# The queries of the last attention block: made in that block from stored transposed rows, and no longer in the block before

## The chip, the cores and the metric

One Trainium2 chip, and on it one core. The time of a run is the device time of that core in microseconds. The kernel before took 2020.83 us, the median of 9 runs (2013.94 to 2037.01).

The names of the engines are those of the profile: PE multiplies matrices, PEld loads the stationary operand of a matmul, DVE is the vector engine, ACT the scalar engine with its table functions, POOL issues the indirect DMAs (gathers and scatters by an index list), SP issues plain DMAs. PSUM is the memory that PE writes to, in banks of 512 float32 per partition.

## The reference

A graph network of four layers on 3327 nodes with 256 features. `adj` is a random sparse matrix with ones on its diagonal; a node of this input has itself and at most 24 others as neighbours. Three of the layers are attention blocks, the second one is an average over neighbours.

```python
def _L3_gnn_ref(x, adj, w_qkv, w_proj, b_proj, w1, b1, w2, b2, g1, be1, g2, be2):
    qkv = layer_norm(x, g1, be1) @ w_qkv                 # [n, 768]
    qkv = qkv.reshape(n, 3, HEADS, HEAD_DIM)             # 8 heads of 32
    q, k, v = (qkv[:, 0], qkv[:, 1], qkv[:, 2])
    scores = jnp.einsum('nhd,mhd->hnm', q, k) * SCALE    # SCALE = 32 ** -0.5
    scores = jnp.where(adj != 0, scores, -jnp.inf)
    out = jnp.einsum('hnm,mhd->nhd', softmax(scores), v).reshape(n, DIM)
    x = x + out @ w_proj + b_proj
    ff = gelu(layer_norm(x, g2, be2) @ w1 + b1) @ w2 + b2   # 256 -> 1024 -> 256
    return x + ff

x = _L0_gnn_ref(x, adj, ...)   # attention
x = _L1_gnn_ref(x, adj, ...)   # h = x @ Wt.T; average of neighbours' h with softmax weights; norm
x = _L2_gnn_ref(x, adj, ...)   # attention
x = _L3_gnn_ref(x, adj, ...)   # attention
```

## The kernel before

The nodes, sorted by their number of neighbours, are cut into 26 tiles of 128 rows. Tile t has room for `ROOM[t]` neighbours per node, from 24 down to 4. The stages, with their places in the trace: neighbour lists out of `adj` (to about 280 us), the first attention block (to 720), the averaging layer (to 1021), the middle attention block (to 1553) and the last one (to the end). In the code the three attention blocks are `layer` 0, 1 and 2, and they run the same functions.

A block works tile by tile in the order written in `GROUPS[layer]`, in which one to four tiles make a group. For a tile, `attend` (L1282) does this:

- It loads the tile's own row of queries, keys and values into `own`, a part of a buffer `first`. In the last block that is a load on SP from the DRAM table `own[t]` (L1294).
- ACT copies the 256 query columns into `query`, half a PSUM bank (L1297). There are two such halves (`QS` is 2).
- POOL gathers keys and values of the neighbours, one indirect DMA per neighbour slot, four slots to a buffer (`first`, then `unit`s). DVE multiplies each buffer's keys by `query` and reduces them to `scores`. In the trace these are the groups `first<-first,query` and `unit<-unit,query`.
- ACT takes the exponential, DVE weights the values and adds them up in `acc` and then `o`, and PE transposes `o` into `turns`.

`project` multiplies by `w_proj` and adds to the rows `x`. A few tiles later `norm`, `turned` and `feed_forward` make `hT` (normed, transposed rows; a ring of two buffers, `HTS`), the sixteen w1 matmuls with their gelu `gT`, and the eight w2 matmuls of a tile. `end` closes the tile. In the last block it scatters the rows of `x` to the output. In the middle block it calls the `finish` of `into_keys` (L985), which makes what the last block needs: the next layer's norm and its transposed rows `hT`, two matmuls 512 wide for keys and values and a copy to `qkv`, two matmuls 256 wide for queries and a scaled write beside them (L1004 and L1005), a scatter of keys and values on POOL into the table from which the last block gathers, and a store of the whole row (768 float32) on SP to `own[t]` (L1010). A float32 matmul of the program appears in the trace as two, so that one tile's keys and values are four instructions of PE there, and its queries four more. `mm` is the ring of three PSUM banks that all these matmuls write to, and L402 and L406 are the lines of a helper through which all instructions of the blocks go, so that groups are told apart by their tiles' names.

The order on each engine is planned. The blocks' code only records operations (`Weave.record`); `order` (L289) then plays them through with a modelled duration for each, picks at each step the operation that can start first (of several, the one of the earlier tile), hands out the buffers of the rings, and adds a slack where an operation waits for another engine's: 8.0 us where DVE waits for PE (`SLACK` for tensor to vector), 1.0 for PE to ACT, 0.6 for ACT to DVE, and 0.1 for pairs that aren't listed. `emit` writes the operations in that order, and each engine then runs its own list in order, waiting where a semaphore says so.

The gathers of the last block wait for all scatters of the middle block (`held = making`).

Of the kernel before, what the change touches and what calls it, by code (L numbers as in the profile page):

```python
# [32 lines left out]
P = 128  # L33
CW = 512
N = 3327
DIM = 256
# [4 lines left out]
SCALE = HD**-0.5  # L41
# [11 lines left out]
KC = DIM // P  # L53
# [15 lines left out]
SLACK = {("tensor", "vector"): 8.0, ("tensor", "scalar"): 1.0, ("scalar", "vector"): 0.6, ("scalar", "gpsimd"): 6.0, ("vector", "gpsimd"): 6.0, "unit": 2.0, "first": 2.0}  # L69
# [25 lines left out]
OTS, HTS, XHS, OS, QKVS = 2, 2, 3, 4, 2  # L95
# [89 lines left out]


class Op:
    __slots__ = ("spots", "lane", "method", "args", "kw", "then", "rank", "needs", "busy", "done", "table", "n", "moves", "alone")


class Weave:
# [33 lines left out]
    def record(self, lane, method, args, kw, then, alone, also):  # L225
        op = Op()
        op.lane, op.method, op.args, op.kw, op.then = lane, method, args, kw, then
        op.n = len(self.ops)
        op.rank, op.alone = self.rank, alone
        op.moves = False  # L230
# [24 lines left out]
        self.cost(op, *plain)  # L255
        self.ops.append(op)
        return op
# [31 lines left out]
    def order(self):  # L289
        ops = self.ops  # L290
# [12 lines left out]
        ready = [0.0] * len(ops)  # L303
# [25 lines left out]
        table, flights, starts, clock = 0, [], {}, Clock()  # L329
        while len(starts) < len(ops):  # L330
            best = None
            for lane in LANES:
                can = []
                for n in wait[lane]:
                    t = opening(ops[n])
# [16 lines left out]
            op = ops[pick]  # L352
# [24 lines left out]
            for n in users[pick]:  # L377
                left[n] -= 1
                same = ops[n].lane == lane
                end = free[lane] if same and lane == "tensor" else ends[pick]  # L380
                ready[n] = max(ready[n], end + (0.0 if same else SLACK.get((lane, ops[n].lane), 0.1)))
                if not left[n]:
                    wait[ops[n].lane].append(n)
        self.starts, self.length, self.at = starts, max(ends), at
# [27 lines left out]
class Sparse:  # L412
# [572 lines left out]
    def into_keys(self, layer, w_qkv, g1, be1):  # L985

        def then(b):
            w = b.w
            made = []
            rows = b.ring("qkv", [P, 3 * DIM], QKVS)  # L990

            def begin():
                b.keys = self.fetch_keys(w_qkv, g1, be1, w)

            def finish(group, sums):
                wq, g, be = b.keys
                hT = b.turned(group, sums, g, be)
                out = []
                for q, t in enumerate(group):
                    r = rows()  # L1000
                    kv, qq = b.mm(), b.mm()
                    w.tensor.matmuls(kv, [(hT[:, k, ts(q, P)], wq[:, k, DIM : 3 * DIM]) for k in range(KC)])
                    w.scalar.copy(r[:, : 2 * DIM], kv)
                    w.tensor.matmuls(qq[:, :DIM], [(hT[:, k, ts(q, P)], wq[:, k, :DIM]) for k in range(KC)])  # L1004
                    w.scalar.mul(r[:, 2 * DIM :], qq[:, :DIM], SCALE)  # L1005
                    w.gpsimd.indirect_dma_start(
                        out=self.places[layer], out_offset=bass.IndirectOffsetOnAxis(ap=self.half[t], axis=0),
                        in_=r[:, : 2 * DIM], in_offset=None, then=lambda ins: self.apart(ins, made), alone=True,
                    )
                    w.sync.dma_start(out=self.own[t], in_=r)  # L1010
                return out

            self.making = made
            return begin, finish, None

        return then
# [238 lines left out]
class Block:  # L1255
# [26 lines left out]
    def attend(self, t):  # L1282
# [11 lines left out]
            w.sync.dma_start(out=own[:, : 3 * DIM], in_=L.own[t])  # L1294
        query = self.query()
        s = self.scores()[:, : (J + 1) * HEADS].rearrange("p (j h) -> p j h", h=HEADS)
        w.scalar.copy(query, own[:, 2 * DIM : 3 * DIM])  # L1297
        units = []
        held = L.held
        for j0 in range(0, J, UNIT):  # L1300
# [165 lines left out]
    def run(self):  # L1466
        w = self.w
        later = []

        def call(now):  # L1470
            while later and (now is None or later[0][0] <= now):
                at, stage, group, rank, made = later.pop(0)
                w.rank = rank
                if stage == 1:
                    later.append((at + DELAY[1], 2, group, rank, self.feed_forward(group, made)))
                    if self.ahead and group == sum(GROUPS[self.layer][-1], ()):
                        self.ahead(w)
                else:
                    self.end(group, made)
                later.sort(key=lambda x: (x[0], -x[1]))  # L1480

        step = 0
        for squad in GROUPS[self.layer]:
            group = sum(squad, ())
            sums = self.small["sums"]()
            for pair in squad:
                outs = []
                for t in pair:
                    w.rank = step
# [546 lines left out]
```

## Time and profile before

| | |
|---|---|
| median of the 9 runs | 2020.83 us |
| all runs | 2013.94, 2015.85, 2018.14, 2018.59, 2020.83, 2032.62, 2036.69, 2036.99, 2037.01 |
| the profiled execution | 2015.0 us, its span 2013.3 us |
| mean granted clock of TensorE | 0.791 |
| busy in the span | PE 1262.9 us (63%), DVE 1374.5 (68%), POOL 982.3 (49%), PEld 852.3 (42%), ACT 728.3 (36%) |
| the middle block, 1022 to 1553 (531 us) | PE 362.8, DVE 366.6, ACT 234.1, POOL 241.0 |
| the last block, 1553 to 2013 (460 us) | PE 288.8, DVE 347.4, ACT 146.0, POOL 244.5 |

The busy time of an engine is the time in which it executes; PEld runs beside PE. The granted clock is the share of full speed at which the throttle lets TensorE run. In a group of instructions, the numbers after the bar are busy time, mean nanoseconds of one, and the idle time of the engine just before these instructions with what ended it. In a line of waits, the instruction left of the arrow waited for the one right of it: total us, times, longest. In the timeline a line is one instruction, with its start, its duration and, in brackets, what it had waited for.

### The profile page before, as it was taken

To read this page: it belongs to the slowest core of one execution; us is meant where nothing else is said; L and a number is where in the kernel's file an instruction comes from. 1 tells how busy PE (TensorE), PEld (TensorE's weight loads), DVE (VectorE), ACT (ScalarE), POOL (GpSimd) and SP (SyncE) were. 2 spreads that over 40 slices of the span, in tenths; PEclk is the share of its full clock that TensorE was granted. 3 is DMA by queue.
4 is the path that set the end of the run, shared out by engine and by line. 5 is a ranking of instruction groups with operands and counts; after the bars stand their busy time and mean duration, and the time that the engine had idled before them with its cause. 6 is when DMAs were issued, how large, how long until landed. Compare 5 with 4: busy or idle time off the path is not lost. (4 is left out here: it accounts for less than half of the span.)

```text
span 2013.3 us, 18004 instructions
## 1 busy us (share of the span) xinstructions
PE 1262.9 (63%) x5126; PEld 852.3 (42%) x5126; DVE 1374.5 (68%) x3500; ACT 728.3 (36%) x1575; POOL 982.3 (49%) x977
## 2 busy tenths in 40 slices
PE   3335513575765587899924776877687157578775
PEld 1112201252434345666512454555465043345554
DVE  5999338776756792256737786878661699788882
ACT  5654211323323243032312453554454134144332
POOL 6998456556454422011165445545401666656530
PEclk9667755677887688899866888988789577788787
DMA  8987396555454453474486556556513666655620
GB/s 297 374 334 279 119 324 196 169 172 159 147 175 130 139 121 103 110 218 154 190 308 219 175 187 208 189 174 203 156 58 134 208 195 207 206 164 182 166 84 13
DMA packets 166245, 369.77 MB, mean 184 GB/s; under 512 B 75629, under 2 KB 87123, under 8 KB 162808
## 3 DMA queue, kind: packets, MB, share of 16 engines
q0 software_dynamic: 68624, 222.01, 35.6%
q1 hardware_dynamic: 86279, 115.85, 17.2%
q10 hardware_dynamic: 11232, 30.68, 4.1%
q8 instruction: 42, 0.69, 0.1%
q14 instruction: 68, 0.56, 0.1%
HBM read 279.77 MB, written 77.59 MB: 178 GB/s over the span
## 5 line engine op out<-in xcount | busy, mean ns | idle before, releaser
L406 POOL DMA_INDIRECT unit<-kv,ids x372 | 352.6, 948 | 292.8 <-issue 97.5
L402 PE MATMUL mm<-hT,w 128*128 128x256 f32 (+2 forms) x1280 | 343.0, 423 | 138.7 <-issue 64.4
L406 POOL DMA_INDIRECT first<-kv,ids x338 | 319.9, 946 | 212.1 <-issue 113.9
L402 PE MATMUL mm<-w,gT 128*128 128x256 f32 x1248 | 311.8, 403 | 50.6 <-issue 32.2
L402 PEld LDWEIGHTS mm<-hT,w 128*128 128x128 f32 x1280 | 225.3, 213 | 227.7 <-issue 123.1
L402 PEld LDWEIGHTS mm<-w,gT 128*128 128x128 f32 x1248 | 245.1, 202 | 98.7 <-issue 40.5
L406 ACT ACTIVATE gT<-mm,b 128x128 f32<-128x128 f32 (+2 forms) x320 | 133.3, 467 | 276.0 <-remote 163.3
L406 DVE TENSOR_TENSOR first<-first,query 128x1280 f32<-128x1280 f32 x78 | 115.3, 1478 | 142.3 <-DMA first<-kv,ids 58.1
L402 PE MATMUL mm<-wproj,oT 128*128 128x256 f32 x312 | 115.5, 503 | 73.2 <-issue 38.3
L406 PE MATMUL turns<-ident,o 128*128 128x128 f32 x156 | 40.4, 349 | 183.4 <-issue 91.7
L406 DVE TENSOR_REDUCE scores<-first 128x40 f32<-128x1280 f32 x78 | 116.2, 1489 | 41.3 <-ACT scores L406 28.1
L406 DVE SCALAR_TENSOR_TENSOR rows<-mm,rows 128x256 f32<-128x256 f32 x156 | 64.6, 416 | 102.9 <-remote 62.1
L406 DVE TENSOR_TENSOR unit<-unit,query 128x1024 f32<-128x1024 f32 (+3 forms) x120 | 115.7, 964 | 27.1 <-DMA first<-kv,ids 15.7
L406 DVE TENSOR_TENSOR acc<-acc,unit 128x512 f32<-128x512 f32 (+1 forms) x204 | 131.6, 645 | 1.6 <-DVE scores L406 1.4
L406 DVE TENSOR_REDUCE scores<-unit 128x32 f32<-128x1024 f32 (+3 forms) x120 | 117.6, 980 | 14.9 <-ACT scores L406 8.6
L959 PE MATMUL kvps<-wqkv,hT 128*128 128x512 f32 x208 | 110.9, 658 | 22.6 <-ACT st L962 9.7
L406 DVE TENSOR_TENSOR unit<-unit,scores 128x1024 f32<-128x1024 f32 (+3 forms) x120 | 116.3, 971 | 0.0
L406 ACT ACT_TABLE_LOAD x89 | 114.2, 1283 | 1.5
L1205 POOL DMA_INDIRECT sorted<-unit,to x26 | 24.8, 955 | 182.8 <-ACT unit L963 151.3
L402 PEld LDWEIGHTS mm<-wproj,oT 128*128 128x128 f32 x312 | 71.0, 247 | 98.3 <-issue 46.8
L674 DVE MAX8 found<-m 128x8 f16<-128x416 f16 x208 | 104.9, 577 | 10.4 <-POOL m L660 5.2
L406 PEld LDWEIGHTS turns<-ident,o 128*128 128x128 f32 x156 | 22.8, 173 | 202.4 <-issue 123.7
(215 smaller groups left out, 2211.4 us busy)
## 6 DMA issues: line engine op xcount, KB each, us to landing
a<-in_adj SPq DMA_DIRECT2D x25, 1663.5 KB
kv<-unit ACTq DMA_DIRECT2D x26, 512.0 KB
first<-sorted SPq DMA_DIRECT2D x26, 512.0 KB
own<-qkv SPq DMA_DIRECT2D x26, 384.0 KB
first<-own SPq DMA_DIRECT2D x26, 384.0 KB
kv<-st ACTq DMA_DIRECT2D x13, 512.0 KB
adj<-a SPq DMA_DIRECT2D x15, 416.0 KB
w<-in_L_gnn_w SPq DMA_DIRECT2D x6, 1024.0 KB
```

Of the source, the lines that this page charges most:

```text
L402: self.nc.tensor.matmul(out, real(left), real(right), start=k == 0, stop=k == len(pairs) - 1)
L406: ins = getattr(getattr(self.nc, op.lane), op.method)(*args, **kw)
L674: nc.vector.max(found[:, t, s, :], m[:, ts(s, SEG)])
L959: nc.tensor.matmul(kv, hT[:, k, ts(q, P)], w[:, k, DIM : 3 * DIM], start=k == 0, stop=k == KC - 1)
L1205: nc.gpsimd.indirect_dma_start(out=self.sorted[:], out_offset=bass.IndirectOffsetOnAxis(ap=self.to[:, c + q : c + q + 1], axis=0), in_=y, ...
```

## The change

The finish of the middle block makes keys and values only. The buffer `qkv` shrinks from 768 to 512 columns, the 256-wide matmuls and the scaled write go, and in place of one store of the row there are two: keys and values into the first 512 columns of `own[t]`, and the tile's part of `hT` into the last 256. What then lies in those columns is the transposed rows of the tile, cut into two halves of 128.

In the last block `attend` no longer copies the query. Two matmuls of the program (four in the trace) take the stored halves as stationary operand and the query part of `w_qkv` as moving one and write straight into the PSUM half `query`. The factor SCALE goes into those weights, by one multiplication on ACT that `run` records ahead of the last block's first tile. Each of these matmuls is marked `prompt`, and `order` then lets DVE follow after a slack of 0.1 instead of 8.0 us. The first two blocks copy their queries as before.

```diff
 class Op:
-    __slots__ = (..., "moves", "alone")
+    __slots__ = (..., "moves", "alone", "prompt")
...
@@ order
-                ready[n] = max(ready[n], end + (0.0 if same else SLACK.get((lane, ops[n].lane), 0.1)))
+                ready[n] = max(ready[n], end + (0.0 if same else 0.1 if ops[pick].prompt else SLACK.get((lane, ops[n].lane), 0.1)))
...
@@ into_keys
-            rows = b.ring("qkv", [P, 3 * DIM], QKVS)
+            rows = b.ring("qkv", [P, 2 * DIM], QKVS)
 
             def begin():
                 b.keys = self.fetch_keys(w_qkv, g1, be1, w)
+                self.wq = b.keys[0][:, :, :DIM]
...
-                    kv, qq = b.mm(), b.mm()
+                    kv = b.mm()
                     w.tensor.matmuls(kv, [(hT[:, k, ts(q, P)], wq[:, k, DIM : 3 * DIM]) for k in range(KC)])
-                    w.scalar.copy(r[:, : 2 * DIM], kv)
-                    w.tensor.matmuls(qq[:, :DIM], [(hT[:, k, ts(q, P)], wq[:, k, :DIM]) for k in range(KC)])
-                    w.scalar.mul(r[:, 2 * DIM :], qq[:, :DIM], SCALE)
+                    w.scalar.copy(r, kv)
...
-                    w.sync.dma_start(out=self.own[t], in_=r)
+                    w.sync.dma_start(out=self.own[t][:, : 2 * DIM], in_=r)
+                    w.sync.dma_start(
+                        out=self.own[t][:, 2 * DIM :].rearrange("p (k w) -> p k w", k=KC), in_=hT[:, :, ts(q, P)]
+                    )
...
@@ attend
-        w.scalar.copy(query, own[:, 2 * DIM : 3 * DIM])
+        if layer < 2:
+            w.scalar.copy(query, own[:, 2 * DIM : 3 * DIM])
+        else:
+            ask = w.tensor.matmuls(query, [(own[:, ds((2 * KC + k) * P, P)], L.wq[:, k, :]) for k in range(KC)])
+            ask.prompt = True
...
@@ run
+        if self.layer == 2:
+            w.scalar.mul(self.L.wq, self.L.wq, SCALE)
         for squad in GROUPS[self.layer]:
```

More of the change, by code (lines that the diff above doesn't have):

```diff
@@ L187 @@
 class Op:
-    __slots__ = ("spots", "lane", "method", "args", "kw", "then", "rank", "needs", "busy", "done", "table", "n", "moves", "alone")
+    __slots__ = ("spots", "lane", "method", "args", "kw", "then", "rank", "needs", "busy", "done", "table", "n", "moves", "alone", "prompt")
 class Weave:
@@ L229, in record @@
         op.rank, op.alone = self.rank, alone
-        op.moves = False
+        op.moves, op.prompt = False, False
         outs = [kw[k] for k in ("out", "accum_out") if kw.get(k) is not None]
@@ L1000, in finish @@
                     r = rows()
-                    kv, qq = b.mm(), b.mm()
+                    kv = b.mm()
                     w.tensor.matmuls(kv, [(hT[:, k, ts(q, P)], wq[:, k, DIM : 3 * DIM]) for k in range(KC)])
-                    w.scalar.copy(r[:, : 2 * DIM], kv)
-                    w.tensor.matmuls(qq[:, :DIM], [(hT[:, k, ts(q, P)], wq[:, k, :DIM]) for k in range(KC)])
-                    w.scalar.mul(r[:, 2 * DIM :], qq[:, :DIM], SCALE)
+                    w.scalar.copy(r, kv)
                     w.gpsimd.indirect_dma_start(
                         out=self.places[layer], out_offset=bass.IndirectOffsetOnAxis(ap=self.half[t], axis=0),
-                        in_=r[:, : 2 * DIM], in_offset=None, then=lambda ins: self.apart(ins, made), alone=True,
+                        in_=r, in_offset=None, then=lambda ins: self.apart(ins, made), alone=True,
                     )
-                    w.sync.dma_start(out=self.own[t], in_=r)
+                    w.sync.dma_start(out=self.own[t][:, : 2 * DIM], in_=r)
+                    w.sync.dma_start(
+                        out=self.own[t][:, 2 * DIM :].rearrange("p (k w) -> p k w", k=KC), in_=hT[:, :, ts(q, P)]
+                    )
                 return out
```

## The prediction

> **What bounds the kernel now.** I read the page first (span, stages, chain), then the busy time in windows over the last two attention blocks, then the timeline where they meet, then groups and waits. The profiled execution took 2015.0 us around a span of 2013.3; the median of the runs shown, 2020.83, is 5.8 above it (five runs lie at 2014 to 2021 with mean 2017.5, four at 2032 to 2037).
>
> The edit touches the middle block (from about 1022 us to 1553) and the last one (1553 to the end). Windows, columns PE, PEld, DVE, ACT, POOL busy us (instructions), granted clock, DMA share, GB/s:
>
> ```profile
> 1400.00:1450.00 50.00, 29.00 (x128) 21.85 (x126) 34.98 (x84) 16.46 (x42) 26.23 (x28) 0.83 0.55 170
> 1450.00:1500.00 50.00, 42.04 (x196) 31.45 (x197) 36.47 (x113) 29.97 (x79) 5.16 (x8) 0.86 0.27 90
> 1500.00:1553.00 53.00, 46.00 (x225) 32.89 (x223) 11.93 (x73) 26.13 (x77) 5.57 (x11) 0.97 0.30 107
> 1600.00:1650.00 50.00, 27.00 (x94) 18.58 (x94) 44.56 (x95) 16.14 (x35) 30.24 (x32) 0.70 0.65 208
> 1650.00:1700.00 50.00, 32.05 (x78) 15.64 (x78) 44.95 (x97) 18.38 (x39) 29.00 (x29) 0.68 0.57 177
> 1850.00:1900.00 50.00, 39.15 (x160) 30.13 (x159) 43.55 (x88) 16.64 (x36) 31.55 (x33) 0.87 0.61 168
> ```
>
> So two regimes. Inside a block DVE leads (44 of 50 us) and PE has a third of its time free. At the end of the middle block DVE has run dry (11.93 of 53) and PE is full (46 of 53). The timeline shows that end:
>
> ```profile
> 1488.51 0.42 DVE L406 TENSOR_TENSOR o<-acc,o 128x256 f32<-128x256 f32 x1
> ...
> 1503.68 0.27 PE L406 MATMUL turns<-ident,o 128*128 128x128 f32 x1
> ...
> 1541.95 2.85 PE L402 MATMUL mm<-wqkv,hT 128*128 128x512 f32 x8 [0.55 <-ACT hT L406]
> ...
> 1548.70 4.54 PE L402 MATMUL mm<-wqkv,hT 128*128 128x512 f32 x8 [0.55 <-ACT hT L406]
> ...
> 1552.79 0.96 POOL L406 DMA_INDIRECT kv<-qkv,ids  x1 [6.88 <-ACT qkv L406]
> ...
> 1556.52 0.98 POOL L406 DMA_INDIRECT first<-kv,ids  x1 [2.78 <-issue]
> ```
>
> The last attention row o is done at 1488.9, PE turns it only at 1503.7 (it is behind), and the last keys and values are scattered at 1552.8. The first gather of the last block waits for all scatters. These 63.9 us are on the path that sets the end. (x8 is one tile: four matmuls 512 wide for keys and values, four 256 wide for queries.)
>
> ```profile
> L402 PE MATMUL mm<-wqkv,hT 128*128 128x256 f32 x104 | 28.2, 394 | 2.1 <-ACT qkv L406 1.5 <-DVE acc L406 0.5
> L406 ACT ACTIVATE qkv<-mm 128x256 f32<-128x256 f32 x26 | 9.9, 379 | 21.6 <-remote 14.3 <-PE mm L402 7.0 <-issue 0.3
> L406 ACT COPY query<-first 128x256 f32<-128x256 f32 x43 | 16.3, 379 | 77.9 <-DVE unit L406 26.7 <-DVE first L406 13.4 <-issue 12.5
> ```
>
> The first two groups are what leaves the middle block; the third holds the copies that leave the last.
>
> **The change, part by part.**
>
> *Query matmuls leave the middle block.* A tile's eight matmuls take 2.85 us at the high clock; by width the queries are a third, 0.95. 26 tiles: 24.7 us of PE. Where PE has room this is worth nothing; in the tail it counts. I counted the PE instructions that stand, in the order of the two built programs, between the last o and the last key/value matmul, and priced them with tail rows (key/value tile 1.90, eight w2 matmuls 3.62, sixteen w1 matmuls 3.84, transpose 0.21, projection matmul 0.5, bias 0.28). Before: 6 key/value tiles, 6 query tiles, 4.5 x 3.62, 4 x 3.84, 18 transposes, 4 projections, 7 biases: 57 us, which took 63.9. After: 5 key/value tiles, 3.5 x 3.62, 3 x 3.84, 14 transposes, 2 projections, 5 biases: 39 us. That is 18 less; 5.7 are queries, the rest is feed-forward that now stands ahead of the last o. It has room there: PE work ahead of the last o also falls, from 284 to 277 us. Bounds: 6 if only the queries go (the surplus stands, but PE reaches it as late as now), 18 if all does. What is late next is the last tile's own chain (projection, norm, feed-forward, norm, keys), which doesn't shrink. I take 14, nearer the count, since in before the trace stood within a matmul or two of its listed order at the last o.
>
> *Scaled query writes leave ACT.* 26 x 379 ns = 9.9 us, about 19 of them ahead of the tail where ACT is 40 to 60% busy, each behind the key/value copy that the scatter needs, so not on the path. A PSUM bank per tile is also freed. Gain 0 to 7; counted 0.
>
> *Stores.* One 3 KB-row store per tile becomes two, 2 KB rows and two 512-byte runs per partition: 26 more SP issues at 0.32 us, 8.3 us on a queue that mostly waits (131.4 us for ACT qkv, 130.4 for DVE o). New is that hT is free only once its store has landed, and the store stands in SP's queue behind loads that wait for DVE (longest 25.4). The ring has two hT; who needs the next waits on ACT, and with it the exp behind. Bounds 0 to 12 (about half of that longest wait; the trace has no store of hT). In the tail the DMA is 30% busy and no such load stands between: 0. In the body DVE idles 87 us for many reasons now; I take 0 net with ACT's gain, range -7 to +12.
>
> *Scaling the weights.* One ACT pass over 128x512, 0.58 us like the copy of that shape. In the built order it stands on ACT at the start of the middle block, after the second query copy, waiting for the weight load. That load was issued at 1022.9, ahead of the tile load for which ACT idles 8.98 us until 1037.7. Cost 0; if the weights landed last, its 0.6.
>
> *Queries in the last block.* 26 x 379 ns leave ACT. PE gains 26 x 0.95 = 24.7 us at the high clock, 26 x 1.51 = 39 at the low one (4.54/3, the tile at 1548.70). PE has about 115 us free in 1600 to 1950, so its time alone costs nothing. The new wait is DVE's first multiply of a tile for PE, whose queue it shares with feed-forward. Cover: in the built order the DVE work between a query and its use is mostly 10 to 16 us, but 4 and 8 at the tenth and ninth tile and none at the last but one, where sixteen w2 matmuls stand ahead. Against that, ACT no longer stands at query copies:
>
> ```profile
> ACT query L406 <- DVE unit L406: 23.7, 6, 11.3
> ...
> ACT query L406 <- DVE first L406: 13.4, 2, 12.0
> ```
>
> PE stands there instead, though usually already behind a transpose of o. In this block DVE shows no stall over 1 us that ended with an ACT query, so nothing direct is won. The four first queries lie under the 8 us until the first gather lands. Bounds -10 (all of ACT's 9.9 us) to +25 (PE the bound); I take +4: 3 at the last but one, 1 at the tenth.
>
> The clock bears on this: it is granted at 0.97 in the tail that loses the matmuls, and at 0.70 and 0.68 in two windows that get them. The Trainium skill (TensorE: Matmul & The Clock Gate, Part 1) says that an idle window of some 3.4 us puts PE back at half rate, so it speaks against moving work from a dense to a sparse stage. The trace agrees in kind; by the rule alone every query would run cold and the sum would take the 39 us as PE's added load instead of 24.7, still inside PE's free time.
>
> *The prompt flag* only tells the planner that DVE may follow these matmuls after 0.1 instead of 8 us; its effect is the order counted above.
>
> **Sum.** 2015.0 - 14 + 0 + 4 = 2005 for an execution like the profiled one. Less 10, the lower group's mean gives 2007.5 and the median 2010.8; I forecast 2009.
>
> **Rivals.**
>
> *A, slower: PE's queue becomes DVE's start.* If PE runs more than one tile's cover (about 10.5 us of DVE work) behind its listed place, each tile of the last block begins with a wait. For it: PE waits of 11.4 us for gT in that block, and 15 us at the last block-1 rows turned. Against: PE is a third idle. Price, if PE paces all 26 tiles: 26 x 1.23 (midway between 0.95 and 1.51) = 32, less 14: +18, about 2036.
>
> *B, same: only the query matmuls leave the tail.* PE reaches the last o as late as now; -6, +4, and a few us for held hT: about 2019.
>
> *C, faster still.* ACT, free of copies that wait for DVE, serves gelu and exp sooner in both blocks: -18, -5 in the last block instead of +4: about 1995.
>
> *D, it does not do what it says*: queries are still made once per tile and no fewer matmuls run in all; that is so, and is why only their place counts.
>
> **How the numbers follow.** Forecast 0.50, A 0.21, B 0.18, C 0.11. About 0.5% (10 us) is what a measurement of this kernel tells from none. The forecast's own range is 2000 to 2018, so of its 0.50 some 0.37 is faster. With C and a little of B: faster 0.50. Same takes 0.13 from the forecast, most of B and 0.02 of A: 0.30. Slower 0.20. The range reaches from C to A: 1994 to 2035.
>
> **What would show it.** Right: no 256-wide wqkv matmuls in the middle block; last o to last scatter some 50 us instead of 64; 104 matmuls into query after it; DVE gaps before the first multiply of a tile ended by PE of 3 us or less, except at the last but one tile. Wrong: the scatter-to-end stretch (460 us) grown by more than 10; ACT hT waiting for a DMA of own; the last o much later than 1489.

## The result and the profile after

The changed kernel took 2050.91 us, the median of 20 runs (2041.11 to 2066.4), where the kernel before took 2024.47, the median of 62. The ratio is 1.016, with a 95% interval of 1.0139 to 1.0182: it is slower by 1.6%, some 32 us. (That ratio is of the means of the runs that count as fast, 2053.4 over 2021.0; the medians as they stand differ by 26 us.) The forecast was 2009, its range 1994 to 2035.

The profiled execution has a span of 2043.8 us against 2013.3. The trace can be cut at three events that both kernels have: the first and last attention row of the middle block, the last scatter of its keys and values, and the first and last attention row of the last block. (The events are the starts of DVE's second addition into o, and the start of the scatter, in the timeline.)

| us | before | after | difference |
|---|---|---|---|
| middle block, first o to last o | 439.7 | 450.6 | +10.9 |
| last o to last scatter | 64.3 | 52.3 | -12.0 |
| last scatter to first o of the last block | 24.2 | 24.5 | +0.3 |
| last block, first o to last o | 392.8 | 424.0 | +31.2 |
| last o to the end | 43.4 | 43.4 | 0 |

So the end of the middle block became shorter by about what was forecast, the same block lost nearly as much ahead of it, and the last block lost 31. The end of the middle block, in the timeline of the changed kernel (the same events as were shown of the kernel before):

```profile
1499.63 0.42 DVE L406 TENSOR_TENSOR o<-acc,o 128x256 f32<-128x256 f32 x1
...
1504.20 0.38 PE L406 MATMUL turns<-ident,o 128*128 128x128 f32 x2
...
1540.23 1.98 PE L402 MATMUL mm<-wqkv,hT 128*128 128x512 f32 x4
...
1547.23 3.78 PE L402 MATMUL mm<-wqkv,hT 128*128 128x512 f32 x4 [0.55 <-ACT hT L406]
...
1551.91 0.96 POOL L406 DMA_INDIRECT kv<-qkv,ids  x1 [7.72 <-ACT qkv L406]
...
1555.63 0.98 POOL L406 DMA_INDIRECT first<-kv,ids  x1 [2.76 <-issue]
```

PE turns both halves of the last o 4.2 us after it is done, and only four matmuls stand for a tile. In the kernel before, PE turned the first half 8.8 us after o was done and the second, which the prediction's line shows, 14.8 us after, with feed-forward matmuls between them and no gap of PE's:

```profile
1497.69 0.33 PE L406 MATMUL turns<-ident,o 128*128 128x128 f32 x1
1497.86 3.62 PE L402 MATMUL mm<-w,gT 128*128 128x256 f32 x16
...
1501.89 1.95 PE L402 MATMUL mm<-hT,w 128*128 128x128 f32 x16
1503.68 0.27 PE L406 MATMUL turns<-ident,o 128*128 128x128 f32 x1
```

But o comes at 1499.6 and not 1488.5. The windows of the changed kernel (PE, PEld, DVE, ACT, POOL busy, granted clock, DMA share, GB/s):

```profile
1500.00:1553.00 53.00, 42.30 (x203) 29.74 (x202) 12.06 (x76) 23.81 (x71) 5.24 (x9) 0.93 0.35 123
1600.00:1650.00 50.00, 32.08 (x110) 22.11 (x110) 40.34 (x87) 14.41 (x30) 26.94 (x30) 0.72 0.59 182
1650.00:1700.00 50.00, 30.04 (x62) 15.72 (x63) 41.66 (x91) 11.51 (x28) 26.23 (x26) 0.59 0.54 170
1900.00:1950.00 50.00, 28.76 (x117) 22.37 (x117) 24.98 (x50) 7.36 (x18) 16.38 (x18) 0.78 0.30 85
```

In 1600 to 1700 DVE is busy for 82.0 us, where it was 89.5 in the kernel before; PE has 36 and 40% of its time free there, and the loss is there all the same. In 1900 to 1950 DVE has half its time idle. DVE's waits in the last block, before and then after (waits, total us, times, longest):

```profile
DVE scores L406 <- ACT scores L406: 21.0, 2, 12.4
DVE rows L406 <- remote: 20.9, 6, 5.6
DVE first L406 <- DMA first<-kv,ids: 17.9, 1, 17.9
DVE rows L406 <- PE mm L402: 14.0, 2, 7.0
```

```profile
DVE rows L406 <- PE mm L402: 32.3, 5, 14.6
DVE first L406 <- DMA first<-kv,ids: 18.8, 1, 18.8
DVE first L406 <- remote: 14.1, 2, 7.3
DVE rows L406 <- remote: 11.9, 2, 6.0
DVE first L406 <- PE query L402: 10.1, 2, 8.8
DVE scores L406 <- ACT scores L406: 9.2, 2, 5.2
```

By groups, the idle time ahead of the first multiplies (first<-first,query) went from 19.4 to 52.9 us and that ahead of the additions to rows from 34.9 to 44.8; the waits of scores for ACT fell by 12. The sum, +33.5 + 9.9 - 12, is the 31 us. The two groups, before and then after:

```profile
L406 DVE TENSOR_TENSOR first<-first,query 128x1280 f32<-128x1280 f32 x26 | 38.4, 1478 | 19.4 <-DMA first<-kv,ids 17.9 <-ACT hT L406 1.1 <-DMA unit<-kv,ids 0.2
L406 DVE SCALAR_TENSOR_TENSOR rows<-mm,rows 128x256 f32<-128x256 f32 x52 | 21.5, 415 | 34.9 <-remote 20.9 <-PE mm L402 14.0
```

```profile
L406 DVE TENSOR_TENSOR first<-first,query 128x1280 f32<-128x1280 f32 x26 | 38.5, 1480 | 52.9 <-DMA first<-kv,ids 18.8 <-remote 14.1 <-PE query L402 10.1
L406 DVE SCALAR_TENSOR_TENSOR rows<-mm,rows 128x256 f32<-128x256 f32 x52 | 21.4, 417 | 44.8 <-PE mm L402 32.3 <-remote 11.9 <-PE query L402 0.6
```

Of the first multiplies that wait for a query, the two that wait longest are at 1606.76 and 1940.80. The second is the last but one tile, where the prediction put its 3 us:

```profile
1930.87 3.72 PE L402 MATMUL mm<-w,gT 128*128 128x256 f32 x16
...
1934.73 3.72 PE L402 MATMUL mm<-w,gT 128*128 128x256 f32 x16
...
1938.87 1.89 PE L402 MATMUL query<-wqkv,first 128*128 128x256 f32 x8
```

```profile
1940.80 1.49 DVE L406 TENSOR_TENSOR first<-first,query 128x1280 f32<-128x1280 f32 x1 [8.77 <-PE query L402]
```

The w2 matmuls of two tiles stand ahead of the query, as in the built order, and DVE waits 8.77 us. The first one, at the block's fifth tile, is of another kind, and was not forecast at all. That tile's own query had ended at 1583.77. What DVE waits for is the query of the next tile. PE runs it at 1588.52, for 1.94 us; DVE comes to its multiply at 1599.5 and still waits:

```profile
1588.52 1.94 PE L402 MATMUL query<-wqkv,first 128*128 128x256 f32 x4
```

```profile
1599.05 0.42 DVE L406 TENSOR_TENSOR o<-acc,o 128x256 f32<-128x256 f32 x1 [1.18 <-issue]
1606.76 1.49 DVE L406 TENSOR_TENSOR first<-first,query 128x1280 f32<-128x1280 f32 x1 [7.28 <-remote]
```

PE's signal for that matmul is recorded at 1606.7, 16 us after its record ends. By the name remote the profile says that it finds no record for the releaser.

So two things meet here, a wait for the next tile's query and a late signal. The first is there in every trace of the change. The two halves that `query` takes in turn lie in one PSUM bank. In the last block of none of the twenty traces does a multiply by a query overlap in time with a matmul (or, where ACT makes it, a copy) that writes a query to that bank; where the order of the program puts the next tile's query first, the multiply waits for it. (Tile and query are matched by the semaphores of the tiles' loads, which both wait for.) In this trace eight first multiplies wait for PE, 34 us in sum, when their own query has been over for 0.9 to 24 us: four start 0.04 us after the record of the next one ends, four 1.6 to 16 us after it. No run puts the halves into two banks. The late signal is what the sections below turn on.

### The profile page after: what moved, and what is told of

Same layout as the page of the kernel before. It is cut to its first block, busy times and chain, and to the rows that moved or that the text cites. A ratio compares the mean times of both kernels' runs of the same rounds, so it can differ in the third digit from the quotient of the medians.

```text
span 2043.8 us, 17999 instructions
## 1 busy us (share of the span) xinstructions
PE 1267.7 (62%) x5126; PEld 855.0 (42%) x5126; DVE 1374.5 (67%) x3500; ACT 707.2 (35%) x1520; POOL 982.4 (48%) x978
```

## The experiments

**Two kinds of chips.** The experiments ran on seven chips. On one kind the kernel before takes 2003 to 2057 us, on the other 1727 to 1743 (but for one run of 3077). In all six traces from the first kind, those of the two kernels shown here among them, PE's signals come late: counted are signals that are recorded more than 3 us after a matmul that signals has ended by its record. There are 60 such cases in the first trace of the kernel before (520 us in sum, longest 35) and 50 to 61 in the other five. In the fourteen traces from the second kind there is none; there each signal is recorded within 0.02 us of a record's end. So the two kinds are told apart below as chips with late and with prompt signals, and each ratio of an experiment is against the kernel before on the same chip. No chip was met twice, so whether the kind belongs to the chip or to the moment isn't shown.

The count needs a caution. The traces of the late kind also lack records of signals, and not PE's alone: the first one has 683 records for 769 signalling instructions of PE, 2142 for 2945 of DVE, 868 for 1161 of ACT, where the prompt ones lack none. So some of the 60 may only be unrecorded, and DVE and ACT have some 50 to 75 cases by the same count. But for these two nearly every signal so counted is the prompt one of a later instruction: only 8 of DVE's 64 and none of ACT's 54 stand at no instruction's end (within 0.1 us), against 48 of PE's 60. And at 46 of PE's 60 an instruction of ACT or DVE starts within 0.15 us, after its engine had stood idle for over 0.5 us. The starts alone say the same. Where ACT stood idle for the turned o, it began up to 23 us after PE's record on the late kind, and 1.1 us at most on the prompt one; where PE stood idle for o, it began up to 3.8 us after DVE's record, and 0.3.

The same place of the same program, the changed kernel, on both kinds. First late (PE, then ACT and DVE):

```profile
1856.57 0.66 PE L406 MATMUL tr<-ident,xh 128*128 128x128 f32 x4
1857.06 0.38 PE L406 MATMUL turns<-ident,o 128*128 128x128 f32 x2
...
1868.00 1.22 PE L402 MATMUL mm<-wproj,oT 128*128 128x256 f32 x2 [7.97 <-ACT oT L406]
```

```profile
1866.67 1.02 ACT L406 ACTIVATE hT<-tr,be,g 128x256 f32<-128x256 f32 x2 [16.41 <-remote]
1867.58 0.37 ACT L406 COPY oT<-turns 128x256 f32<-128x256 f32 x1
```

```profile
1866.61 0.42 DVE L406 SCALAR_TENSOR_TENSOR rows<-mm,rows 128x256 f32<-128x256 f32 x1 [5.88 <-remote]
```

Then prompt (the run after_third; PE, then ACT):

```profile
1590.20 0.66 PE L406 MATMUL tr<-ident,xh 128*128 128x128 f32 x4
1590.69 0.38 PE L406 MATMUL turns<-ident,o 128*128 128x128 f32 x2
```

```profile
1590.89 1.02 ACT L406 ACTIVATE hT<-tr,be,g 128x256 f32<-128x256 f32 x2 [7.00 <-PE tr L406]
```

ACT follows the transposes after 0.7 us on the one, after 10.1 on the other, where DVE is released within 0.1 us of ACT. PE itself then stands 8 us for ACT.

**The parts, one at a time.** Four kernels, and the two of the case again.

e1 is the changed kernel with the last block of the kernel before:

```diff
-        if layer < 2:
-            w.scalar.copy(query, own[:, 2 * DIM : 3 * DIM])
-        else:
-            ask = w.tensor.matmuls(query, [(own[:, ds((2 * KC + k) * P, P)], L.wq[:, k, :]) for k in range(KC)])
-            ask.prompt = True
+        w.scalar.copy(query, own[:, 2 * DIM : 3 * DIM])
...
-        if self.layer == 2:
-            w.scalar.mul(self.L.wq, self.L.wq, SCALE)
```

> The middle block is that of the changed kernel (keys and values only, two stores), the last block that of the kernel before: it copies what lies in the query columns on ACT. Those columns hold transposed rows here, so the attention weights of the last block are not the reference's; all work is there but for the 26 query products. Theory 1 (the loss lies in the last block, where DVE's first multiply waits for a query that PE makes late; the middle block keeps the gain of its shorter end): 10 to 14 us below the kernel before, ratio 0.993 to 0.995. Theory 2 (the middle block gives its gain back before its end, by hT held by the new store or by another wait): ratio 0.999 to 1.003, and the last attention row o of the middle block stands some 10 us later than in the kernel before.

> The middle block changed, the last one as before (queries copied; its attention weights are not the reference's, since the copied columns hold transposed rows; 26 query products left out). It is to be seen once more because the first run of it fell on a chip on which the kernel before takes 1735 us. Where PE's signals are late (kernel before near 2020 to 2040 us): theory 1, the loss of the changed kernel lies in the last block: 0 to 14 us below the kernel before, ratio 0.993 to 1.000. Rival, the middle block shares in the loss: ratio 1.003 to 1.008. On a chip with prompt signals: 1.000 as measured.

e2 is the changed kernel with the middle block of the kernel before: `finish` as it was, with the 256-wide matmuls, the scaled write and one store of the row.

> The middle block is that of the kernel before (queries made, scaled and stored with keys and values), the last block that of the changed kernel: PE multiplies the stored 256 columns, which are no transposed rows here, by the scaled weights, so the attention weights of the last block are not the reference's. Theory 1: the whole loss of the last block without the gain of the middle one, 30 to 45 us above the kernel before, ratio 1.015 to 1.022. Theory 2 (the middle block gives nothing): the same as the changed kernel within 5 us, ratio 1.014 to 1.018. If the loss were in the middle block: ratio below 1.005.

> The last block changed, the middle one as before (its attention weights are not the reference's). Where PE's signals are late: theory 1: ratio 1.015 to 1.025, and DVE's waits ahead of the first multiply of a tile, ended by PE or by a late signal, sum to 25 us or more against none in the kernel before. Rival, half of the loss or more belongs to the middle block: ratio 1.004 to 1.009. On a chip with prompt signals: 1.006 as measured.

e4 changes the order in the last block alone:

```diff
             ask.prompt = True
+            ask.rank = -1
```

> The changed kernel with the query matmuls put ahead of all other PE work that is ready, in the planner (their rank is -1). Theory 1, with the queue of PE as the cause (the query stands behind feed-forward matmuls): most of the waits of DVE's first multiplies go, and the time falls by 15 to 30 us, ratio to the kernel before 0.999 to 1.009. Rival: the queries wait for their half bank or for the row's load and not for PE's queue, or PE, standing at an early query, makes the feed-forward late instead: no more than 8 us below the changed kernel, ratio 1.012 to 1.018.

> The changed kernel with its query matmuls planned ahead of other PE work. On the chip with prompt signals it took as long as the kernel before (1.000). Where signals are late: if the place in PE's queue is what costs, the same here, ratio 0.997 to 1.005; if each signal from PE to DVE costs by its lateness wherever it stands, the loss stays, ratio 1.010 to 1.018.

> The changed kernel with its queries planned first, a third time, for a chip with late signals from PE (kernel before near 2020 to 2040 us): ratio 0.997 to 1.005 if the place in PE's queue is what costs, 1.010 to 1.018 if a wait of DVE on PE costs by the lateness of the signal. Prompt signals: 0.998 to 1.000 as twice before.

> The changed kernel with its queries planned first. On a chip with late signals from PE: ratio 0.997 to 1.005 if the queries' place in PE's queue is what costs there too; 1.010 to 1.018 if a wait of DVE on PE costs by the lateness of the signal, wherever the query stands. Prompt signals: 0.998 to 1.000 as three times before.

e5 is the kernel before with the work and without the wait:

```diff
         w.scalar.copy(query, own[:, 2 * DIM : 3 * DIM])
+        if layer == 2:
+            w.tensor.matmuls(self.mm()[:, :DIM], [(own[:, ds((2 * KC + k) * P, P)], L.wq[:, k, :]) for k in range(KC)])
...
```

The weights are scaled once there too. The edit adds more than PE's time: the matmuls take turns in the ring mm, and the planned order of the last block is another one, DVE's from its 61st instruction after the last scatter on.

> The kernel before, whose last block copies the stored queries on ACT as before and beside that runs the same two query matmuls a tile on PE, into a bank of mm that nobody reads (and scales the weights once). It adds the work on PE and leaves out that DVE waits for it. Theory 1 (the dependence, not the work): at most 8 us above the kernel before, ratio 1.000 to 1.004. Rival (PE's added work, 25 to 39 us in a cold block, delays the feed-forward and with it the rows): 15 to 35 us above, ratio 1.008 to 1.017.

> The kernel before with the same query matmuls beside its copies, into a bank that nobody reads. On a chip with late signals: ratio 1.000 to 1.004 if only the dependence costs; 1.008 to 1.017 if the work on PE does, or the later signals of the work queued behind it. Prompt signals: 1.001 as before.

> The changed kernel itself, beside the runs of one call in which the kernel before took 1735 us and not 2024, and in which PE's signals came without the bursts that the first two traces show. If the loss of 1.6% belongs to the waits of DVE on PE's late signals (theory 1), it shrinks where the signals are prompt: ratio 1.000 to 1.006. If it belongs to the changed order of the work (rival), it stays at 1.014 to 1.018 wherever the kernel runs.

> The kernel before, for its trace beside that of the changed kernel on the same chip. Where its time is near 1735 us, its DVE is expected to be busy over 90% from the middle of the blocks on, with no wait for an ACT or PE result over 5 us; where it is near 2020, the waits of the first trace come back.

> The changed kernel beside the parts. Late signals: 1.013 to 1.018 as before. Prompt signals: the two parts' ratios 1.000 and 1.006 multiply to 1.006, so 1.004 to 1.008, and e4's order alone is worth 0.6%.

Measured, as ratios to the kernel before with 95% intervals:

| | prompt signals | late signals |
|---|---|---|
| changed kernel | 1.0041 (1.0021 to 1.0062) | 1.016 (1.0139 to 1.0182), 1.0157 (1.0076 to 1.0237) |
| e1, middle block alone | 1.0002 (0.9985 to 1.0019), 0.9991 (0.9969 to 1.0014) | not run |
| e2, last block alone | 1.0062 (1.0039 to 1.0085), 1.0057 (1.0036 to 1.0077) | not run |
| e4, queries first | 0.9997 (0.9978 to 1.0015), 0.9987 (0.9964 to 1.0011), 0.9992 (0.9969 to 1.0015) | 1.0229 (1.0172 to 1.0286) |
| e5, work without wait | 1.0008 (0.9987 to 1.003) | 1.0108 (1.0055 to 1.0161) |

And the stretches of the traces, in us:

| | middle, first o to last o | last o to last scatter | last block, first o to last o |
|---|---|---|---|
| prompt: e5 | 345.5 | 63.9 | 336.9 |
| prompt: e1 | 356.6, 354.4 | 52.1, 52.0 | 332.7, 332.4 |
| prompt: e2 | 343.9, 344.0 | 62.8, 62.3 | 341.5, 340.9 |
| prompt: changed kernel | 355.0 | 52.5 | 341.5 |
| prompt: e4 | 354.9, 353.1, 353.3 | 52.8, 51.9, 52.9 | 334.3, 333.7, 334.2 |
| late: kernel before | 439.7, 431.2 | 64.3, 63.5 | 392.8, 401.3 |
| late: changed kernel | 450.6, 451.2 | 52.3, 52.9 | 424.0, 443.0 |
| late: e4 | 460.1 | 52.0 | 429.1 |
| late: e5 | 447.8 | 63.9 | 418.0 |

Three things follow.

The middle block gives nothing. Its stretch ahead of the last o is 10 us longer and its end 11 us shorter, with prompt signals as with late ones (e1 against e5, whose middle blocks are those of the changed kernel and of the kernel before). The first forecast for e1 (10 to 14 us below) failed, and theory 2 held in its outcome, with the last o some 10 us later. For e2 both theories had expected 1.014 or more; with prompt signals it is 1.006.

In the last block, with prompt signals, the queries cost 8.7 us (341.2 against 332.5, the means of e2 and e1), and most of it is DVE's waits for them. The groups of e1, of the changed kernel and of e4 there, first multiplies (busy, mean ns, idle time ahead and what ended it):

```profile
L406 DVE TENSOR_TENSOR first<-first,query 128x1280 f32<-128x1280 f32 x26 | 38.5, 1482 | 19.0 <-DMA first<-kv,ids 18.7 <-issue 0.2
```

```profile
L406 DVE TENSOR_TENSOR first<-first,query 128x1280 f32<-128x1280 f32 x26 | 38.5, 1481 | 26.0 <-DMA first<-kv,ids 18.7 <-PE query L402 7.2
```

```profile
L406 DVE TENSOR_TENSOR first<-first,query 128x1280 f32<-128x1280 f32 x26 | 38.5, 1482 | 20.0 <-DMA first<-kv,ids 18.4 <-PE query L402 1.4 <-PE mm L402 0.2
```

7.2 us ended with a query, that of the next tile each time: 1.2, 1.3, 0.7 and 3.7 us at tiles 4, 13, 20 and 25 of the block, whose own queries had ended 0.9 to 21 us before. Asked first (e4), it is 1.4, and the block is back at 334. So where signals are prompt, nearly the whole cost is when PE gets to these queries. e5's 336.9 don't speak against it: after its last o the kernel needs 39.5 us, the others 41.6 to 44.1, so that the two stretches together are those of e1 within about 1 us.

Where they are late it is not. There e4 has the same group at

```profile
L406 DVE TENSOR_TENSOR first<-first,query 128x1280 f32<-128x1280 f32 x26 | 38.6, 1483 | 58.3 <-remote 30.8 <-DMA first<-kv,ids 18.9 <-PE mm L402 3.9
```

and the kernel as a whole is 2.3% slower. Asking earlier didn't help in that trace: every first multiply but the last stands behind the next tile's query there, and the four waits that end remote, 30.8 us in sum, ended 3 to 13 us after that query's record (21 to 28 after that of their own). Whether e4 is worse there than the changed kernel the runs don't say: 9 us of its trace's loss lie in the middle block, which is the same in both. And e5, in which DVE waits for no query of PE, loses 1.1%, about 22 us of 2022. From the first o of the last block to the end it takes 457 us in the one trace, 12 to 21 more than the kernel before; there ACT's copies of the query come late (20.1 us of DVE's waits; none and 8.3 in the two traces of the kernel before), behind other results of PE that ACT waits for. But the changed kernel has no such copies, and e5's middle block, the same in order as that of the kernel before, is 8 to 17 us longer in this trace as well. So e5 is slower on such a chip without the wait, and what the work, the order and the wait each bring to the 1.6% isn't shown.

**Is it the order or the store?** The changed middle block has both a new store of hT and a new order on every engine. e7 keeps the old order: the query matmuls and the scaled writes are planned as in the kernel before, and left away when the order is written out. DVE and POOL then have exactly the old order in that block, both stores are there, and the last block asks first as in e4.

```diff
@@ emit
+                if op.drop:
+                    continue
@@ into_keys
-            rows = b.ring("qkv", [P, 2 * DIM], QKVS)
+            rows = b.ring("qkv", [P, 3 * DIM], QKVS)
...
-                    kv = b.mm()
+                    kv, qq = b.mm(), b.mm()
...
-                    w.scalar.copy(r, kv)
+                    w.scalar.copy(r[:, : 2 * DIM], kv)
+                    w.tensor.matmuls(qq[:, :DIM], [(hT[:, k, ts(q, P)], wq[:, k, :DIM]) for k in range(KC)]).drop = True
+                    w.scalar.mul(r[:, 2 * DIM :], qq[:, :DIM], SCALE).drop = True
```

> The middle block is planned with the queries as in the kernel before, and only when the order is written out are the query matmuls and the scaled writes left away; so DVE and POOL of that block keep the old order exactly. The last block asks for its queries first, as in e4. Where PE's signals are prompt: the last attention row o stands as early as in the kernel before, the stretch from it to the last scatter loses the query tiles alone (57 us instead of 64), and the last block costs what it did: 5 to 8 us below the kernel before, ratio 0.995 to 0.998. If the 10 us that the changed kernel's middle block loses ahead of its last o came from the new store and not from the new order, they stay: ratio 1.001 to 1.004. Where PE's signals are late: 0.993 to 1.000 if asking first holds there too, 1.005 or more if each query that DVE waits for costs by its lateness.

It fell on a chip with prompt signals: ratio 0.9999 (0.9977 to 1.0021), so the 5 to 8 us that were expected are not there. Windows up to the last o and from it to the last scatter, of e5 (the old middle block), of e1 (the changed one) and of e7:

```profile
816.00:1270.80 454.80, 357.06 (x1524) 251.68 (x1523) 398.61 (x1060) 232.22 (x558) 248.51 (x264) 0.89 0.68 225
1270.80:1335.00 64.20, 57.19 (x292) 42.35 (x290) 13.49 (x82) 30.72 (x92) 7.05 (x13) 0.97 0.33 117
```

```profile
816.00:1282.20 466.20, 358.83 (x1509) 252.79 (x1507) 400.14 (x1064) 227.04 (x553) 250.44 (x267) 0.86 0.68 223
1282.20:1335.00 52.80, 40.76 (x199) 28.45 (x197) 12.17 (x75) 24.48 (x73) 5.24 (x9) 0.93 0.37 124
```

```profile
816.00:1266.10 450.10, 340.51 (x1416) 234.37 (x1414) 394.86 (x1048) 225.95 (x540) 249.23 (x264) 0.88 0.70 228
1266.10:1328.80 62.70, 52.72 (x266) 37.58 (x266) 13.43 (x82) 28.84 (x86) 6.11 (x13) 0.94 0.36 118
```

From its first o to its last e7's middle block takes 344.3 us, as in the kernel before: the store of hT costs nothing there, and the 10 us of the changed kernel are the order's. DVE has 2 us more work between those two events in e1 than in e5 (341.6 against 339.7) and 9 us more idle time (15.0 against 5.9), in waits of up to 2.4 us, 10.7 in sum for ACT's results and 1.8 for PE's. And without the queries the end is 62.6 us long, where the five traces of the old middle block with prompt signals (e5, e2 twice, and e8 twice, which follows) have 62.3 to 63.9: six tiles' query matmuls are worth nothing there that can be seen, and not 6 us. Against e5, PE's busy time falls by 4.5 us and its idle time grows by 3. So the end is not set by how much PE has to do.

**Is it POOL?** The late signals stand where POOL issues gathers: 18 of the 60 of the first trace in the first block, 19 in the middle one, 19 in the last, one in the averaging layer, where PE is busy for 262 of 301 us and POOL for 40, and none in the two ends after a block's last o. Past 280 us, 24 of 57 ended when POOL's last issue was over by 1.5 to 4.5 us, in 39 us of waiting of that kind (counted from the last matmul that waits to signal); 33 ended while POOL issued or sooner after, in 313 us. That is 0.62 and 0.11 per us. The other five traces have 0.52 to 0.62 and 0.10 to 0.13. So a pause of POOL may let a signal through, or may come of the same cause. e8 and e9 were to test it: the kernel before and the changed one, with the last block's gathers as plain loads of the same size from SP, at the old places in the plan.

```diff
...
+                if layer == 2:
+                    row = (UNIT * t + j0 + j) % 40
+                    op = w.gpsimd.dma_start(
+                        out=u[:, j, :], in_=L.places[layer][ds(row * P, P), :], then=lambda ins: L.after(ins, held)
+                    )
+                    op.moves, op.busy, op.done, op.on = True, 1.25, 3.45, "sync"
+                    continue
                 w.gpsimd.indirect_dma_start(
```

> The kernel before, but in its last block the 254 gathers by POOL are plain loads of the same size from the same table, issued by SP at the places where POOL issued them in the plan. They read rows by position and not by neighbour list, so the values of the last block are not the reference's; DMA bytes, DVE, PE and ACT work are the same. On a chip with late signals: if POOL's issuing holds PE's signals back, the last block has at most 4 late signals instead of 16 to 19, and first o to last o takes 330 to 350 us instead of 393 to 401, while the middle block keeps its 17 to 21 late signals. If it is the traffic or the block itself: 15 late signals or more, and 385 us or more. On a chip with prompt signals: no late ones, 325 to 345 us.

> The same exchange of gathers for plain loads in the last block of the changed kernel (values not the reference's). On a chip with late signals: if POOL's issuing is what makes PE's signals late and with them the queries dear, first o to last o of the last block is 5 to 15 us longer than in the kernel before with plain loads, as on a chip with prompt signals (9), and not 31 to 42. If the price has another cause, it stays at 25 us or more.

> The kernel before with the last block's gathers as plain loads from SP (rows by position, so values not the reference's), once more. On a chip with late signals: if POOL's issuing holds PE's signals back, at most 4 late signals in the last block instead of 16 to 19, and 330 to 350 us from its first o to its last instead of 393 to 401; if it is the traffic or the block itself, 15 or more and 385 us or more. Prompt signals: the last block as in the first run of it.

> The changed kernel with the last block's gathers as plain loads (values not the reference's), once more. On a chip with late signals: 5 to 15 us more from first o to last o of the last block than the kernel before with plain loads, if POOL's issuing is what makes the queries dear; 25 us or more if not. Prompt signals: as in the first run of it.

All four fell on chips with prompt signals, so the question stays open. What they gave: e8 0.9982 (0.9961 to 1.0003) and 1.0000 (0.9985 to 1.0015), e9 1.0020 (0.9994 to 1.0046) and 1.0026 (1.0005 to 1.0048); the last block from first to last o 332.3 and 332.4 us in e8, 341.2 and 340.0 in e9. With prompt signals the 8 to 9 us of the queries don't depend on who moves the rows.

## Why the prediction was wrong

- *Query matmuls leave the middle block, -14.* The stretch from last o to last scatter fell by 12, near the 14, and partly by luck. Wrong was the sentence that the surplus feed-forward "has room there" ahead of the last o: PE had, but DVE, which leads there, lost 10.9 us (10 to 11 with prompt signals as well) to small waits in the new order. And of the 12 the queries themselves are none that could be seen (e7), where the prediction counted 5.7 and took 6 as the lower bound: the priced PE work is no measure of a stretch in which PE waits in turn for ACT and DVE. The net of the step is -1. (Its line for the last o turned is that of the second half; PE turned the first 6 us earlier.)
- *Scaled query writes, stores, scaling the weights: 0 each.* Right. e7, with both stores, keeps the old middle block's time. The scaling took 0.63 us on ACT, inside the time in which it would have waited for the tile's load: 4.34 and 4.29 us of idle time on its two sides, 8.98 in one piece before.
- *Queries in the last block, +4.* The place was right, the first multiply of a tile, the last but one above all, and so was the side. With prompt signals the term is +8.7. In the profiled execution it is +31, outside its own bounds of -10 to +25. What failed is the cover: the DVE work between a query and its use was read from the order alone, as if DVE could start when the matmul's record ends. Counted to a tile's own query it was about right: with prompt signals there is no wait at the tenth tile and one of 3.7 us at the last but one, where the prediction had 1 and 3. It left out the next tile's query in the same bank, 3.2 us at three other tiles, and the late signals: in the first trace of the changed kernel the two waits that ended remote, 14.1 us, ended 16 and 7 us after that query's record. For the second the trace of the kernel before held the warning: 20.9 us of DVE's waits at rows ended remote, and in the last block these of ACT:

```profile
ACT gT L406 <- remote: 43.0, 5, 13.0
...
ACT hT L406 <- remote: 19.4, 2, 13.5
```

The prediction cited PE's wait of 11.4 us for gT as a sign of PE's queue; there PE waited for ACT, which had itself waited 12.7 us, remote. So the prediction made a new dependence on PE without adding the lateness that the dependences there were showed. The 15 us at the last rows turned are no such case: PE had no gap there, and with prompt signals (e2) it turns the halves 7.1 and 13.1 us after the same o, so "behind" was right. "Its time alone costs nothing" holds with prompt signals (e5, 1.0008); with late ones e5 is 1.1% slower, for reasons that it doesn't separate. (PE's free time in 1600 to 1950 is 108 us, not 115.)

- *The clock.* PE's query matmuls were busy for 39.6 us (37.7 with prompt signals), not 24.7. A tile's four took 1.03 to 1.13 us at the high clock and 1.91 to 2.08 at the low one, where 13 of the 26 ran, most of them in the first half of the block. The prediction's other sum had 39 us, met by luck: its 1.51 was read from a tile whose matmuls ran partly at the high clock, and 26 tiles at 2.07 would be 54. The rule of the Trainium skill (TensorE: Matmul & The Clock Gate, Part 1), half rate after an idle window, agrees with the two rates. The size was not what set the time: with prompt signals the same matmuls without the wait (e5) leave the time where it was, 1.0008.
- *The rivals.* A was nearest (slower, by the same waits, 2036), but by another mechanism than PE pacing every tile: in the first trace eight of the 26 wait for PE. B, in which only the queries leave the end, would have been no gain at all instead of 6 us. C, that ACT's freedom pays, is not seen: DVE's waits of scores for ACT fell by 12 us in the first trace and grew elsewhere by more. D holds as it stands: both kernels have 5126 matmuls in the trace.

The Trainium skill (PSUM — Partial Sum Buffer, Engine vs sequencer instructions) says that an increment attached to a matmul fires on its completion. The prompt traces agree: each signal is recorded within 0.02 us of a record's end. In the late ones ACT, standing idle, started up to 23 us behind the record's end, so there either the record's end is not the completion or the rule doesn't hold; the runs don't tell which.

No version of these beats the kernel before: e4 and e7 equal it where signals are prompt, and e4 is slower where they are late.

## What to carry to other kernels

When an edit gives the bound engine a new producer to wait for, read first how late that producer's results already come to others (waits that end remote, or with a matmul that was done long before) and add that to each new wait; work that is hidden by the order of instructions alone need not be hidden if its signal is late. Here a stretch that several engines fill in turn got no shorter when one of them lost work, and work that was moved ahead of it was paid where it went: ask whether the engine that leads there has room, and not only the engine that does the work. When two buffers of a ring share a PSUM bank, see in the trace whether a reader of the one waits for the writer of the other. And compare only kernels that ran on the same chip.

## What was not expected of the hardware

The same program takes 1735 us on some chips and 2020 to 2036 on others, 16 to 17% more, with DVE's work equal (busy 1374.5 us in the first trace, 1368 to 1370 in those of 1721 to 1745, all versions together). The mean granted clock is 0.78 to 0.80 there and 0.83 to 0.85 on the others, and which of the two differences follows from the other isn't shown. What the slower chips show in addition are late signals of PE: 50 to 61 a run by the count above, up to 36 us each, many at the same places of the program each time, some of them released in bursts (five signals between 1866.58 and 1866.84 for matmuls of 1856.4 to 1859.7 in the first trace of the changed kernel). They stand where POOL issues gathers one behind the other and end four to six times as often, per us of waiting, in a pause of POOL. That POOL holds them back is not shown, and why other chips don't do it is open.
